# A Macaron block with routed experts: routing steps one to a unit, projections earlier, expert passes shifted

## The chip, the cores and the metric

The kernel runs on one core of a Trainium2 chip. The metric is the device time of one execution in microseconds, the median of several runs. In this text PE is TensorE's matmul side and PEld its weight loads, DVE is VectorE, ACT is ScalarE, POOL is GpSimd and SP is SyncE.

## What is computed

Eight sequences of 512 tokens with 128 features go through a feed-forward half, an attention and a second feed-forward half with the same weights:

```python
x = x + 0.5 * _L0_ffn_ref(_layernorm(x), ...)
x = x + _L0_attn_ref(_layernorm(x), w_qkv, w_o, log_xi)
x = x + 0.5 * _L0_ffn_ref(_layernorm(x), ...)      # the same weights as the first
```

The feed-forward part is a mixture of 8 experts of width 512, of which each token takes the best 2:

```python
logits = jnp.einsum('bsd,de->bse', x, router_w) + router_b
topk_scores, topk_idx = jax.lax.top_k(logits, 2)
topk_gates = jax.nn.softmax(topk_scores, axis=-1)
...
    h = jax.nn.relu(jnp.einsum('bsd,df->bsf', x, w1) + bb1)      # for each expert
    y = jnp.einsum('bsf,fd->bsd', h, w2) + bb2
    acc = acc + y * c[..., None]                                 # c: the token's gate, or 0
```

The attention is causal, with 16 heads of width 8, a rotation on some head types and a distance decay on others. All is float32.

## The kernel before

**Groups and rooms.** Tokens are sent to their experts through DRAM. The sequences form three groups ahead of the attention (f0: 0 and 1; f1: 2 to 4; f2: 5 to 7) and three behind it (g0: 0 to 2; g1: 3 to 5; g2: 6 and 7). For each group, `route` finds every token's two experts and its place, and 8 scatters a sequence (GpSimd's indirect DMA, line 796) write the normalised tokens to `xs`. `experts` fetches each expert's rows from `xs` (line 854), transposes them (867), multiplies by W1 (876), applies ReLU (883, or 885 on VectorE), multiplies by W2 (900), adds the bias (904) and writes `ys` (907). `combine` gathers each token's two results (968) and adds them to `x` with the gates (955).

**Routing in six steps.** `route` is a generator. Where the layernorm isn't there yet it takes three steps. Then come: 1, four transposes into one PSUM bank and their copy `xnT` by VectorE (713, 715); 2, the router's matmuls (742) and VectorE's comparison of each logit with each other (746 to 760); 3, rank and mask (763, 765); 4, the count of earlier tokens by matmuls on the mask (770 to 778), the places, and the entry of the eight scatters in the queue of transfers; 5 and 6, the gates.

**Units.** The program is an order written out by hand: PE, ACT, DVE and SP run their instructions as they are issued. Time is cut into numbered units. Units 0 to 95 each hold one step of attention: sequence b, group g of four heads, step s of three; a sequence is 12 units. `surround(n, att)` (1278) issues one unit: the scores of unit n (1059) and their exponentials (1066), the values of unit n-1 (1085), one piece of expert work, the causal minimum (1073), one transfer, the outputs, the additions due, then all streams due in this unit, each followed by its share of expert pieces, and a second transfer if the queue is long or holds an urgent one. The units before 0 and after 97 have no attention in them. An expert pass of a group is 65 or 73 pieces; a piece is one transposition, one W1 product of a block or one W2 product of a tile. The pieces of a pass are spread evenly over the units that `plan` gives it (1272): (group, unit of the fetch, first unit, end).

**Streams.** `at(u, stream, steps, each)` (1256) puts `each` steps of a stream into each unit from u on. `routed` puts the three steps of a layernorm into a unit each, then the six of the routing two to a unit: transposes with the router's matmuls, mask with the count, the gates together. `project(b)` has nine steps: layernorm, transposes, the projection's matmuls in two parts, the rotation on GpSimd in two parts, and the copies into `qpad` and `kpad` (1023, 1026). `operands(b, g)` transposes one head group of `qpad` and `kpad` into `qT` and `kT` (1036, 1042), in two steps. `finish(b)` ends the attention of b, and the routing for the second half begins two units after that.

**Buffers.** In units 0 to 97, PSUM has four banks for scores, one for values, and three named `m` that all else takes in turn: expert pieces, transposes, the router's logits, counts, outputs. The queue of transfers holds scatters and gathers in order; each is also held back until the last marked instruction issued before it is done (`behind_mark`).

**The start.** Sequences 0, 1 and 2 are normalised and routed by a list of steps ahead of the first unit (lines 1326 to 1335). Sequence 3 is normalised there, and routed in unit `first`, together with the first expert's pieces.

Of the kernel before, what the change touches and what calls it, by code (L numbers as in the profile page):

```python
# [22 lines left out]
T = N // P  # L23
# [452 lines left out]
class Main:  # L476
# [127 lines left out]
    def behind_mark(self, ins):  # L604
        if self.mark is not None:
# [3 lines left out]
                reason="transfers kept apart",  # L609
            )  # L610

    def transfer(self, second=False):

        if self.jobs and (
            not second or len(self.jobs) > 4 or any(urgent for urgent, _ in self.jobs)
        ):
            self.jobs.popleft()[1]()
# [108 lines left out]
        g.seen = const.tile([P, E], BF, name=f"seen_{key}")  # L726
        return g

    def route(self, g, i, urgent=False):

        nc, small, tc = self.nc, self.small, self.tc
        b = g.seqs[i]
# [71 lines left out]
            self.behind_mark(ins)  # L804
            g.placed += 1

        for t in range(T):
            for r in range(2):
                self.jobs.append((urgent, partial(scatter, t, r)))

        with nc.allow_low_precision(reason="counts of at most 32, exact in bf16"):
            by_e = mask.rearrange("p t e -> p e t")
# [133 lines left out]
    def combine(self, g, i, dst=None, urgent=False, ahead=False):  # L946

        nc = self.nc
        b = g.seqs[i]
        x = self.x[b]  # L950
        self.whole[b] = False

        def add(t, yts):
            for r in range(2):
                nc.vector.scalar_tensor_tensor(  # L955
                    x[:, t, :], yts[r], g.gates[:, i, t, r : r + 1], x[:, t, :],
                    ALU.mult, ALU.add,
                )
            if t == T - 1:
                self.whole[b] = True  # L960
                if dst is not None:
                    nc.sync.dma_start(dst[b].rearrange("(t p) d -> p t d", p=P), x)

        yts = {}

        def gather(t, r):
            yt = self.yp.tile([P, D], FP, tag=f"yt{r}", name=f"yt_{g.key}_{b}_{t}_{r}")
            self.pool.indirect_dma_start(
                out=yt[:, :], out_offset=None, in_=g.ys[:, :],
                in_offset=bass.IndirectOffsetOnAxis(  # L970
                    ap=g.back[:, i, t, r : r + 1], axis=0
                ),
            )
            yts[t, r] = yt
            if r == 1:
                self.adds.append((self.unit + 2, partial(add, t, [yts[t, 0], yts[t, 1]])))

        new = [(urgent, partial(gather, t, r)) for t in range(T) for r in range(2)]
        if ahead:
            self.jobs.extendleft(reversed(new))  # L980
        else:
            self.jobs.extend(new)
        yield


# [144 lines left out]
    def verdict(self, bad):  # L1130

        nc = self.nc
        nr = B * G * T * 4
        flat = self.recs.rearrange("p b g t h -> p (b g t h)")
        spare = self.p1.tile([P, T * 3 * D], FP, tag="qkv", name="spare")
        okay, wok = spare[:, : nr + 3 * D], spare[:, nr + 3 * D : nr + 6 * D]
        nc.vector.tensor_scalar(okay[:, :nr], flat, 1.0 / SUM_LIMIT, None, ALU.is_ge)
        nc.vector.scalar_tensor_tensor(
            okay[:, :nr], flat, SUM_LIMIT, okay[:, :nr], ALU.is_le, ALU.mult
        )  # L1140
        nc.vector.tensor_scalar(wok, self.wqkv_sb, -W_LIMIT, None, ALU.is_ge)
        nc.vector.scalar_tensor_tensor(
            okay[:, nr:], self.wqkv_sb, W_LIMIT, wok, ALU.is_le, ALU.mult
        )
        cnt = self.const.tile([P, 1], FP, name="okay_cnt")
        nc.vector.tensor_reduce(cnt, okay, AX.X, ALU.add)
        cp = self.bank([P, 512], "okay_ps")
        nc.tensor.matmul(cp[:1, :1], cnt, self.ones_f, start=True, stop=True)
        over = self.const.tile([1, 1], FP, name="over")
        nc.vector.tensor_reduce(  # L1150
            over, self.counts.rearrange("o k e -> o (k e)"), AX.X, ALU.max
        )
        nc.vector.tensor_scalar(over, over, 0.5, None, ALU.is_gt)
        nc.vector.scalar_tensor_tensor(
            bad, cp[:1, :1], float(P * (nr + 3 * D)) - 0.5, over, ALU.is_lt, ALU.max
        )


@with_exitstack
def macaron_kernel(  # L1160
# [22 lines left out]
    bad = flags.tile([1, 1], I32, name="bad")  # L1183

    def run(*streams):
        for s in streams:
            for _ in s:
                pass
# [23 lines left out]
    with ExitStack() as main:  # L1212
        m = Main(tc, main, aps)
# [4 lines left out]
        f0 = m.open_group([0, 1], 384, 0, "f0")  # L1218
        f1 = m.open_group([2, 3, 4], 512, 1, "f1")
        f2 = m.open_group([5, 6, 7], 512, 2, "f2")  # L1220
        g0 = m.open_group([0, 1, 2], 512, 1, "g0")
        g1 = m.open_group([3, 4, 5], 512, 2, "g1")
        g2 = m.open_group([6, 7], 384, 0, "g2")
        order = [f0, f1, f2, g0, g1, g2]
        place = {True: {}, False: {}}
# [13 lines left out]
        def step(*streams):  # L1239
            for st in streams:  # L1240
                next(st, None)
# [8 lines left out]
        units = [(b, g, s) for b in range(B) for g in range(G) for s in range(len(m.STEPS))]  # L1250
        per = len(m.STEPS)
        seq = G * per
        first, core, tail, ends = -28, len(units), 111, 127
        due = {}

        def at(u, stream, steps, each=1):

            for k in range(0, steps, each):
                due.setdefault(u + k // each, []).append((stream, min(each, steps - k)))

        def routed(u, g, i, urgent=False):
            r = m.route(g, i, urgent)
            if g is not f1:
                at(u, r, 3)
                u += 3
            at(u, r, 6, 2)

        def combined(u, g, i, dst=None, urgent=False, ahead=False):
            at(u, m.combine(g, i, dst, urgent, ahead), 1)


        plan = [
            (f0, first, first, -15), (f1, -17, -15, 7), (f2, 5, 7, 41), (g0, 50, 52, 86),
            (g1, 85, 87, tail - 1), (g2, tail - 2, tail - 1, ends),
        ]
        fills = {}

# [46 lines left out]
        with m.banks(("m", 8)):  # L1324

            n = [m.normalise(b) for b in range(5)]
            r = [m.route(f0, 0), m.route(f0, 1), m.route(f1, 0)]
            step(n[0], n[0], n[1], n[1], n[0], n[0])
            step(r[0], n[1], n[1], r[0], r[1], r[0], r[0])
            transfers(8)  # L1330
            step(r[1], r[1], r[1], n[2], n[2], n[3], n[3], n[4], n[4])
            transfers(8)
            step(r[0], r[0], r[1], r[1], n[2], n[2], r[2], n[3], n[3], r[2], n[4], n[4], r[2], r[2])
            transfers(8)
            run(*r, *n)
            m.bias_columns()

            routed(first, f1, 1, urgent=True)
            routed(first + 2, f1, 2, urgent=True)
            routed(first + 1, f2, 0, urgent=True)  # L1340
            combined(-15, f0, 0, urgent=True, ahead=True)
            routed(-15, f2, 1, urgent=True)
            combined(-11, f0, 1)
            routed(-8, f2, 2, urgent=True)
            at(-9, m.project(0), 9)
            at(-1, m.operands(0, 0), 2, 2)
            for b in range(B):
                u = b * seq
                if b == 2:
                    combined(8, f1, 0, urgent=True)  # L1350
                elif b > 2:
                    combined(u - (19 if b == 5 else 20), *place[True][b], urgent=b == 5)
                if b > 0:
                    at(u - (9 if b == 1 else 10), m.project(b), 9)
                for g in range(G):
                    v = u + g * per
                    if g == 0 and b > 0:
                        at(v - 1, m.operands(b, g), 2, 2)
                    elif g > 0:
                        at(v - 2, m.operands(b, g), 2)  # L1360
                at(u + seq + 2, m.finish(b), 2)
                routed(u + seq + 4, *place[False][b], urgent=b in (2, 5, 7))
            for i in range(3):
                combined(87, g0, i, out, urgent=True)
                combined(tail, g1, i, out, urgent=True)

            for u in range(first, 0):
                surround(u, False)
                if u == first:
                    m.attention_constants()  # L1370
                    m.load_x(5, 6, 7)
                    m.clear(2)
        with m.banks(("st", 1), ("o", 1), ("m", 3)):
            for u in range(core + 2):
# [1 line left out]
        with m.banks(("m", 8)):  # L1376
            for u in range(core + 2, ends):
                surround(u, False)
                if u == tail:
                    m.verdict(bad)  # L1380
            run(fills["g2"][0])
            assert not due, due
            for i in range(2):
                run(m.combine(g2, i, out))
            m.mark = None
            while m.jobs:
                m.transfer()
                m.unit += 1
                m.additions()
            m.unit += 2  # L1390
            m.additions()
# [53 lines left out]
```

## Time and profile before

| | |
|---|---|
| time, median of 3 runs | 830.54 us (830.22 to 835.65) |
| span of the profiled run | 828.3 us |
| the chain that ended last, by engine | PE 74%, DVE 13%, DMA 4%, POOL 3%, issue 3%, ACT 2% |
| first and second product of the experts, busy | 199.8 us (876), 196.1 us (900) |
| scores and values, busy | 103.8 us (1059), 93.4 us (1085) |
| exponentials, busy | 158.7 us (1066) |
| indirect transfers on GpSimd, busy, the four costliest groups | 231.2 us |

The profile cuts the span into 40 slices of 20.7 us. Each digit is the share of a slice in tenths, 9 standing for 90% or more; PEclk is the TensorE clock that was granted.

```profile
PE   3178999789989789889969879979989979978950
DVE  6645135534345555654675545656645454522322
PEclk9999999989989889889978989989999999998985
```

PE starts slowly in the first two slices, is near full from the fourth on, and is done before the last. Its clock dips in many of the slices in between. The slices about number 20 (400 to 440 us) are the attention units that have no expert pieces in them.

### The profile page before, as it was taken

The numbers are of one execution on the slowest core, as the hardware profiler recorded it, in microseconds if no ns is written. First come the engines' busy times: TensorE is split into PE (matmuls) and PEld (weight loads), VectorE is DVE, ScalarE is ACT, GpSimd is POOL, SyncE is SP. The second block draws the span as 40 slices with busy tenths as digits, with TensorE's granted clock in tenths as the row PEclk, the third lists the DMA queues.
The fourth block names the chain that finished last, engine by engine and source line by source line (L and its number), as shares of the span: only waits on it lengthen the run. The fifth ranks groups of instructions, "written<-read, shape, count | busy, mean of one in ns | idle before, by whom it ended". The sixth has DMA issues, their size and how long they took to land.

```text
span 828.3 us, 12920 instructions
## 1 busy us (share of the span) xinstructions
PE 683.3 (82%) x4867; PEld 432.9 (52%) x4867; DVE 409.8 (49%) x1351; ACT 346.3 (42%) x520; POOL 317.2 (38%) x352
## 2 busy tenths in 40 slices
PE   3178999789989789889969879979989979978950
PEld 2157766556555446546524545545646546755840
DVE  6645135534345555654675545656645454522322
ACT  4023434345636245345435435534545535323410
POOL 4743556540232242243362233324214224542734
PEclk9999999989989889889978989989999999998985
DMA  9762333111211010101102011101002112322522
GB/s 298 242 215 67 102 97 102 39 39 52 58 46 32 14 45 26 29 27 32 33 23 78 17 35 46 45 10 36 21 13 77 52 45 77 103 87 64 134 70 64
DMA packets 74005, 55.77 MB, mean 67 GB/s; under 512 B 7088, under 2 KB 66768, under 8 KB 73936
## 3 DMA queue, kind: packets, MB, share of 16 engines
q1 hardware_dynamic: 65456, 38.08, 15.5%
q0 software_dynamic: 8192, 16.79, 7.0%
q8 instruction: 40, 0.66, 0.3%
q14 instruction: 29, 0.24, 0.1%
q10 hardware_dynamic: 288, 0.01, 0.0%
HBM read 27.07 MB, written 27.79 MB: 66 GB/s over the span
## 4 chain that ended last, share of the span: by engine, by line
PE 74%; DVE 13%; DMA 4%; POOL 3%; issue 3%; ACT 2%; POOLq 0%; DVEq 0%; SPq 0%
PE st L1059 11%; PE z_g L876 10%; PE y_g L900 10%; PE y_f L900 10%; PE z_f L876 9%; PE o L1085 9%; PE qkv_ps_a L998 3%; DVE ee L1073 3%; DVE x L955 2%; PE qT_ps L1036 2%; PE kT_ps L1036 1%; DMA yt_g<-ys,back_g 1%; PE xbT_ps_g L867 1%; PE otok_ps L1103 1%; PE lg_ps_f L742 1%
## 5 line engine op out<-in xcount | busy, mean ns | idle before, releaser
L1066 ACT ACTIVATE ee<-st 128x768 f32<-128x768 f32 (+1 forms) x192 | 158.7, 879 | 97.0 <-PE st L1059 96.8
L467 POOL DMA_INDIRECT yt_f<-ys,back_f x64 | 64.6, 1009 | 177.7 <-DVE ee L1073 81.4
L1059 PE MATMUL st<-qT,kT 32*128 32x512 f32 (+3 forms) x1024 | 103.8, 499 | 13.5 <-DVE qT L1042 7.5
L900 PEld LDWEIGHTS y_f<-w_sb,h_f 128*128 128x128 f32 x704 | 94.0, 200 | 33.9 <-issue 20.7
L900 PEld LDWEIGHTS y_g<-w_sb,h_g 128*128 128x128 f32 x704 | 89.9, 193 | 34.9 <-issue 18.9
L796 POOL DMA_INDIRECT xs<-xn_g,to_g x64 | 65.5, 1023 | 100.6 <-DVE ee L1073 60.6
L876 PE MATMUL z_f<-xT_f,w_sb 128*128 128x512 f32 (+1 forms) x192 | 100.4, 612 | 2.0 <-DVE ysb_f L904 1.3
L876 PE MATMUL z_g<-xT_g,w_sb 128*128 128x512 f32 (+1 forms) x192 | 99.4, 605 | 1.9 <-DVE ysb_g L904 1.3
L1073 DVE TENSOR_TENSOR ee<-ee,keep 128x256 f32<-128x256 f32 (+1 forms) x192 | 92.3, 505 | 16.6 <-ACT ee L1066 16.6
L900 PE MATMUL y_f<-w_sb,h_f 128*128 128x128 f32 x704 | 100.1, 288 | 0.0
L467 POOL DMA_INDIRECT yt_g<-ys,back_g x64 | 61.8, 965 | 92.2 <-ACT h_g L883 32.9
L900 PE MATMUL y_g<-w_sb,h_g 128*128 128x128 f32 x704 | 96.0, 281 | 0.8 <-ACT h_g L883 0.8
L1085 PE MATMUL o<-ee,vpad 128*32 128x512 f32 (+3 forms) x1024 | 93.4, 461 | 0.0
L883 ACT ACTIVATE h_f<-z_f,b1T 128x512 f32<-128x512 f32 (+1 forms) x82 | 53.0, 646 | 91.5 <-PE z_f L876 91.3
L883 ACT ACTIVATE h_g<-z_g,b1T 128x512 f32<-128x512 f32 (+1 forms) x82 | 52.9, 645 | 74.6 <-PE z_g L876 74.2
L904 DVE TENSOR_TENSOR ysb_g<-y_g,b_sb 128x128 f32<-128x128 f32 x88 | 25.5, 289 | 117.0 <-PE y_g L900 116.9
L904 DVE TENSOR_TENSOR ysb_f<-y_f,b_sb 128x128 f32<-128x128 f32 x88 | 25.3, 288 | 106.8 <-PE y_f L900 102.9
L1059 PEld LDWEIGHTS st<-qT,kT 32*128 32x128 f32 x1024 | 45.9, 195 | 60.8 <-issue 27.7
L1085 PEld LDWEIGHTS o<-ee,vpad 128*32 128x32 f32 x1024 | 24.4, 112 | 56.6 <-issue 30.8
L796 POOL DMA_INDIRECT xs<-xn_n,to_f x40 | 39.3, 982 | 34.1 <-ACT h_f L883 11.5
L1042 ACT COPY kT<-kT_ps 128x512 f32<-128x512 f32 x32 | 18.8, 589 | 54.1 <-PE kT_ps L1036 54.1
L876 PEld LDWEIGHTS z_f<-xT_f,w_sb 128*128 128x128 f32 x192 | 32.5, 207 | 14.7 <-issue 9.5
(174 smaller groups left out, 816.7 us busy)
## 6 DMA issues: line engine op xcount, KB each, us to landing
w_sb<-in_L_ffn_W_dram SPq DMA_DIRECT2D x16, 256.0 KB, 5.8
xs<-zeros SPq DMA_DIRECT2D x2, 2048.0 KB
xb_f<-xs SPq DMA_DIRECT2D x16, 256.0 KB, 3.7
ys<-ysb_f SPq DMA_DIRECT2D x16, 256.0 KB, 2.4
xb_g<-xs SPq DMA_DIRECT2D x16, 256.0 KB, 3.0
ys<-ysb_g SPq DMA_DIRECT2D x16, 256.0 KB, 2.4
x<-in_L_attn_x_dram SPq DMA_DIRECT2D x8, 256.0 KB, 4.4
out_dram<-x SPq DMA_DIRECT2D x8, 256.0 KB, 2.6
```

What stands on the lines that cost most here:

```text
L467: ins = op(*args, **kw)
L796: ins = nc.gpsimd.indirect_dma_start(out=g.xs[:, :], out_offset=bass.IndirectOffsetOnAxis(ap=g.to[:, i, t, r : r + 1], axis=0), in_=xn[:, ...
L876: nc.tensor.matmul(z[:, :n], self.w1_sb[:, e, ts(c, P)], xT[:, n0 : n0 + n], start=True, stop=True,)
L883: ins = nc.scalar.activation(dst, z[:, :n], AF.Relu, bias=bias)
L900: nc.tensor.matmul(y, h[:, c, ts(t, P)], self.w2_sb[:, e, c, :], start=(c == 0), stop=(c == C - 1),)
L904: ins = nc.vector.tensor_tensor(ys[:, t, :], y, self.b2_sb[:, e], ALU.add)
L998: nc.tensor.matmul(pp[:, : 3 * D], xnT[:, ts(t, P)], self.wqkv_sb, start=True, stop=True)
L1036: self.nc.tensor.transpose(tp[:, ts(t, P)], pad[:, t, 4 * g : 4 * g + 4, :].rearrange("p h s -> p (h s)"), self.ident,)
L1059: nc.tensor.matmul(st[:, h, c0 : c0 + N - kt * P], kT[r0 : r0 + SLOT, ts(kt, P)], qT[r0 : r0 + SLOT, kt * P :], start=True, stop=True,)
L1066: nc.scalar.activation(ee[:, two, :width], st[:, two, :width], AF.Exp)
L1073: ins = self.nc.vector.tensor_tensor(d, d, self.keep.unsqueeze(1).unsqueeze(1).to_broadcast([P, 2, len(parts), P]), ALU.min,)
L1085: self.nc.tensor.matmul(self.o[h * SLOT : (h + 1) * SLOT, kt * P :], self.vpads[b % 2][:, kt, 4 * g + h, :], ee[:, h, c0 : c0 + n], start= ...
```

## The change

Only the order of the work changes. No operation of the computation is added or taken out.

- `routed` gives each of the six routing steps a unit of its own, so that the copies and masks that the next matmuls read are made a unit ahead of them. A routing's scatters enter the queue two units later.
- The projections begin a unit or two earlier, and the operands of the first head group are made in the two units ahead of their scores, as for the other groups.
- `first`, `tail`, `ends`, the plan of the expert passes, the combines and their places in the queue are moved to match.
- The fourth sequence (3, the second of f1) is routed as far as its scatters in the list ahead of the first unit. The loads of x for sequences 5 to 7 go ahead of the first expert's fetch.
- The verdict on overflow is issued in two units rather than one.
- The code that enters transfers in the queue is shared by `route` and `combine`; a routing may now go ahead of what is queued.

```diff
+    def enter(self, transfers, urgent, ahead):
+        new = [(urgent, transfer) for transfer in transfers]
+        if ahead:
+            self.jobs.extendleft(reversed(new))
+        else:
+            self.jobs.extend(new)
...
-    def route(self, g, i, urgent=False):
+    def route(self, g, i, urgent=False, ahead=False):
...
-        for t in range(T):
-            for r in range(2):
-                self.jobs.append((urgent, partial(scatter, t, r)))
+        self.enter([partial(scatter, t, r) for t in range(T) for r in range(2)], urgent, ahead)
...
         nc.vector.tensor_reduce(cnt, okay, AX.X, ALU.add)
+        yield
         cp = self.bank([P, 512], "okay_ps")
...
-        first, core, tail, ends = -28, len(units), 111, 127
+        first, core, tail, ends = -29, len(units), 113, 129
...
-        def routed(u, g, i, urgent=False):
-            r = m.route(g, i, urgent)
+        def routed(u, g, i, urgent=False, ahead=False):
+            r = m.route(g, i, urgent, ahead)
             if g is not f1:
                 at(u, r, 3)
                 u += 3
-            at(u, r, 6, 2)
+            at(u, r, 6)
...
-            (f0, first, first, -15), (f1, -17, -15, 7), (f2, 5, 7, 41), (g0, 50, 52, 86),
-            (g1, 85, 87, tail - 1), (g2, tail - 2, tail - 1, ends),
+            (f0, first, first, -16), (f1, -18, -16, 6), (f2, 4, 6, 43), (g0, 52, 54, 89),
+            (g1, 87, 89, tail - 1), (g2, tail - 2, tail - 1, ends),
...
-            r = [m.route(f0, 0), m.route(f0, 1), m.route(f1, 0)]
+            r = [m.route(f0, 0), m.route(f0, 1), m.route(f1, 0), m.route(f1, 1, True)]
...
-            run(*r, *n)
+            step(r[2], r[2], r[3], r[3], r[3], r[3])
+            run(*r[:3], *n)
             m.bias_columns()
-
-            routed(first, f1, 1, urgent=True)
-            routed(first + 2, f1, 2, urgent=True)
-            routed(first + 1, f2, 0, urgent=True)
-            combined(-15, f0, 0, urgent=True, ahead=True)
-            routed(-15, f2, 1, urgent=True)
-            combined(-11, f0, 1)
-            routed(-8, f2, 2, urgent=True)
-            at(-9, m.project(0), 9)
+            m.load_x(5, 6, 7)
+
+            at(first, r[3], 2)
+            routed(first, f1, 2, urgent=True)
+            routed(first, f2, 0, urgent=True)
+            combined(-16, f0, 0, urgent=True, ahead=True)
+            routed(-17, f2, 1, urgent=True)
+            combined(-13, f0, 1)
+            routed(-10, f2, 2, urgent=True)
+            at(-10, m.project(0), 9)
             at(-1, m.operands(0, 0), 2, 2)
             for b in range(B):
                 u = b * seq
                 if b == 2:
-                    combined(8, f1, 0, urgent=True)
+                    combined(6, f1, 0, urgent=True, ahead=True)
                 elif b > 2:
-                    combined(u - (19 if b == 5 else 20), *place[True][b], urgent=b == 5)
+                    combined(u - (17 if b == 5 else 21), *place[True][b], urgent=b == 5, ahead=b == 5)
                 if b > 0:
-                    at(u - (9 if b == 1 else 10), m.project(b), 9)
+                    at(u - 11, m.project(b), 9)
                 for g in range(G):
-                    v = u + g * per
-                    if g == 0 and b > 0:
-                        at(v - 1, m.operands(b, g), 2, 2)
-                    elif g > 0:
-                        at(v - 2, m.operands(b, g), 2)
+                    if b + g > 0:
+                        at(u + g * per - 2, m.operands(b, g), 2)
                 at(u + seq + 2, m.finish(b), 2)
-                routed(u + seq + 4, *place[False][b], urgent=b in (2, 5, 7))
+                routed(u + seq + 4, *place[False][b], urgent=b in (2, 5, 6, 7), ahead=b == 7)
             for i in range(3):
-                combined(87, g0, i, out, urgent=True)
+                combined(89, g0, i, out, urgent=True)
                 combined(tail, g1, i, out, urgent=True)
+            at(tail, m.verdict(bad), 2)
 
             for u in range(first, 0):
                 surround(u, False)
                 if u == first:
                     m.attention_constants()
-                    m.load_x(5, 6, 7)
                     m.clear(2)
...
-                if u == tail:
-                    m.verdict(bad)
```

More of the change, by code (lines that the diff above doesn't have):

```diff
@@ L976, in gather @@
                 self.adds.append((self.unit + 2, partial(add, t, [yts[t, 0], yts[t, 1]])))
[L978 to L982, printed above, removed]
+        self.enter([partial(gather, t, r) for t in range(T) for r in range(2)], urgent, ahead)
         yield
@@ L1156, in verdict @@
         )
+        yield
 @with_exitstack
```

## The prediction

> **What bounds the kernel now.** I read the busy shares first, then the waits of TensorE, then two stretches side by side, then the timeline of one routing.
>
> ```profile
> PE 683.3 (82%) x4867; PEld 432.9 (52%) x4867; DVE 409.8 (49%) x1351; ACT 346.3 (42%) x520; POOL 317.2 (38%) x352
> core 0: 828.3 us, clock 0.925
> ```
>
> TensorE (PE) is the only engine near full, and the clock it was granted averages 0.925. The waits of PE (us in total, times, longest):
>
> ```profile
> PE pos_ps_g L770 <- DVE mask_g L765: 22.5, 8, 3.8
> PE xnT_ps_f L713 <- DVE xn_n L698: 18.5, 2, 11.5
> PE lg_ps_g L742 <- DVE xnT_g L715: 14.6, 8, 2.4
> PE pos_ps_f L770 <- DVE mask_f L765: 13.3, 7, 3.6
> PE qT_ps L1036 <- DVE qpad L1023: 7.8, 2, 5.2
> PE st L1059 <- DVE qT L1042: 7.5, 6, 1.8
> PE lg_ps_f L742 <- DVE xnT_f L715: 7.2, 7, 1.4
> PE okay_ps L1148 <- DVE over L1150: 3.6, 1, 3.6
> ```
>
> Four of the eight rows are the routing, 57.6 us together; each is PE waiting for a VectorE result made in the same unit. What that does to a stretch (columns: PE, PEld, DVE, ACT, POOL busy; granted clock; DMA):
>
> ```profile
> 243.50:265.80 22.30, 22.30 (x197) 13.50 (x196) 14.47 (x48) 12.88 (x18) 3.08 (x4) 1.00 0.12 31
> 270.90:293.00 22.10, 15.96 (x101) 10.16 (x100) 11.73 (x32) 4.57 (x7) 5.07 (x7) 0.81 0.04 10
> 797.80:828.30 30.50, 0.00 (x0) 0.00 (x0) 5.94 (x17) 0.00 (x0) 15.22 (x16) 0.53 0.22 60
> ```
>
> The first holds units 13 to 17: five units with expert pieces and no routing, PE full, full clock, 4.5 us a unit. The second holds two routing units and a little more: PE idle 6.1 us and the clock at 0.81. The third is the end, after the last matmul. Inside the second:
>
> ```profile
> 270.87 0.93 PE L1059 MATMUL st<-qT,kT 32*128 32x384 f32 x8
> 274.12 0.60 PE L713 MATMUL xnT_ps_g<-ident,xn_g 128*128 128x128 f32 x4
> 276.36 0.68 DVE L715 COPY xnT_g<-xnT_ps_g 128x512 f32<-128x512 f32 x1
> 277.09 1.37 PE L742 MATMUL lg_ps_g<-rw_sb,xnT_g 128*128 128x8 f32 x8 [2.38 <-DVE xnT_g L715]
> 282.42 0.94 PE L1059 MATMUL st<-qT,kT 32*128 32x256 f32 x16
> 285.89 1.28 DVE L1073 TENSOR_TENSOR ee<-ee,keep 128x512 f32<-128x512 f32 x2
> 288.20 0.41 DVE L763 TENSOR_REDUCE rank_g<-gt_g 128x32 f32<-128x256 f32 x1
> 288.64 0.25 DVE L765 TENSOR_SCALAR mask_g<-rank_g 128x32 bf16<-128x32 f32 x1
> 288.95 0.21 PE L770 MATMUL pos_ps_g<-mask_g,earlier 128*128 128x32 bf16 x1 [3.77 <-DVE mask_g L765]
> 291.81 2.09 PE L1059 MATMUL st<-qT,kT 32*128 32x512 f32 x8
> ```
>
> The three score rows start units 19, 20 and 21: two units take 20.9 us. The copy and the mask are short (0.68 and 0.66 us); they come late because VectorE is in the middle of the unit's causal minima and additions. PE stands behind them with expert pieces queued that need neither.
>
> **What the Trainium skill says.** "PSUM — Partial Sum Buffer", Engine vs sequencer instructions: ScalarE, VectorE and GpSimd queues are strict FIFO, and matmuls start in program order. The timeline agrees: lg and pos stop everything behind them for 2.38 and 3.77 us. "TensorE: Matmul & The Clock Gate", Part 1: the clock is either full or half, chosen from recent activity in windows of about 3.4 us. The 0.81 beside a full 1.00 agrees, and here waits of 2 to 4 us are enough, less than a whole idle window for some. "Perfetto Trace Analysis", Optimization Strategy: find the gaps of the most-contended engine and make their dependencies start sooner. The same page, Matmuls: independent groups should rotate through PSUM banks so that evacuation overlaps the next group. In the core only three banks rotate, so a late VectorE read can still stop PE; the trace has this twice (z behind ysb at 300 and 495 us, 1.3 us each).
>
> **The change part by part.**
> (a) One routing step per unit. Copy xnT goes into the unit before lg, mask into the unit before pos. No instruction is added. Each result then has the rest of its unit, 2 us and more of expert pieces, and the next unit's scores, values and first piece, about 3 us more: against waits of at most 3.8 us. Of the 57.6 us, 10.0 us are in the prologue before 43 us (0.8, 2.2, 2.7, 0.8, 3.6), where the order of the first three sequences stays. Two more (0.8 and 1.6 us, the fourth sequence) move to (f). That leaves 45.2. VectorE still does the same work, 1.9 us for the comparison chain (0.19 and four of 0.42) in the unit of lg, and holds PSUM banks of pieces behind it; at 0.3 to 0.5 us for each of 20 or so steps I leave 8 us in. Gain 37. Cost on GpSimd: the scatters enter the queue two units later; counting two transfers a unit, they still finish 4 units before the f1 fetch, 4 before f2, 1 or more before g0, g1 and g2, as before.
> (b) Projection sooner. The 7.8 us of qT behind qpad (5.2 for sequence 0, 2.7 for 1) came from writing qpad in the unit that transposes it. Now a unit or more lies between. Gain 7.
> (c) Operands of head group 0 in two units rather than one. qT is copied a unit earlier; kT, copied by ScalarE, now stands just ahead of the scores, as it does for the other groups, whose st waits for kT are 2.8 us in five. Of 10.3 us (7.5 and 2.8) gain 4.
> (d) The verdict in two units: okay_ps no longer waits for its own count. Gain 3 of 3.6; its work moves by nothing else.
> (e) Clock. A mean of 0.925 means 62 us of clock missing in 828.3; the last 30.5 us at 0.53 hold 14 of it and have no matmul. So 48 us in the body. The stretch without expert pieces, 397.5 to 446, has clock 0.79 and so 10 of it, and is partly held by the exponentials there; I count it in (g). From the remaining 38: some lies under idle time already counted[...], so 80%, 30. It hangs on the waits of (a), (b), (d); the wait for the g2 fetch (4.0 us, DMA) and some small gaps stay. I take three quarters: 22.
> (f) Fourth sequence in the prologue. Its transposes, lg and pos (1.1, 1.9, 0.2 us of PE) run where PE waited 4.1 us for the first expert's rows. The chain there, after VectorE has ended the third sequence's gates at 41.0 us: copy 0.7, lg 1.9, VectorE 2.5, pos 0.6, about 47.2 against the 42.75 us at which the first expert's transposes start now: 4.4 us later. It takes out 3.2 us of PE work and 2.4 us of waits behind that. Gain 1. The loads of x for 5 to 7 go ahead of the first fetch on SyncE, which stood idle from 34 to 40 us with the DMA share at 0.20 from 35 to 40: hidden.
> (g) Units 41 to 51 carry no pieces and took 52 us, of which waits of (a) and (c) are 6. The first two ran 3.4 us, 11 times that plus 3 us of routing is 40. Beyond the 6, gain 5.
> Plan bounds, three more units, reordered combines: the pieces and their matmuls are the same 4867, a unit has no cost of its own, and the combine of sequence 5 keeps two units from gather to addition. Nothing.
> Sum: 37 + 7 + 4 + 3 + 22 + 1 + 5 = 79. 830.5 - 79 = 751.5, so **751 us**.
>
> **Rivals.**
> R1, waits turn into new ones: VectorE, 65% busy in a unit of 4.5 us (14.47 of 22.30), holds one of three banks in most of the spread steps, and half the gain goes: about 790. For it: the two z behind ysb waits. Against: units 13 to 17 held a projection's copies with no gap.
> R2, the clock stays low because smaller gaps are enough for it: the waits go, the clock and (g) do not: 751 + 27 = 778. For it: a wait of 1.3 us at 118 us already has 0.87 beside it (115 to 128). Against: full units keep 1.00.
> R3, slower: a later scatter or the tighter combine of sequence 5 (additions end in the unit in which its projection starts, where one gather already held VectorE 2.3 us at 424) stops VectorE, and PE with it, at several boundaries, and the first expert starts later still. At 10 us for each of five fetches and the prologue, with half the gain: 830 - 40 + 60 = 850.
>
> **How the numbers follow.** Forecast 0.66, R1 0.15, R2 0.13, R3 0.04, the rest (better than the sum, all waits and clock gone: 740 and below) 0.02 beyond its own spread. The low end takes the 8 us left in (a), and the quarter of clock left in (e): 751 - 16, 733 with a little of (c). The high end, 787, takes in R2 and the better half of R1. Faster by over 1%: all but R3 and a sliver, 0.94; within 1% 0.02; slower 0.04.
>
> **What would show it.** Right: waits of pos_ps_g and lg_ps_g under 3 us each, qT behind qpad and okay_ps under 1, mean clock 0.95 or more, routing units near 5 us, PE busy around 640 us since fewer matmuls run at half clock. Wrong: new rows of z, y or o behind DVE results of over 15 us in total (R1); waits gone with the clock at 0.93 (R2); waits for xb or x rows (R3).

## The result and the profile after

The changed kernel took 772.63 us (median of 4 runs, 771.14 to 774.20). The ratio to the kernel before is 0.9275, with a 95% interval of 0.9230 to 0.9321. The kernel before took 833.09 us beside it (median of 4 runs). The forecast was 751 us, in a range of 733 to 787: faster as forecast, inside the range, and 22 us above the forecast. Run again with later experiments beside it, the same kernel took 759.40 us, ratio 0.9181 (0.9102 to 0.9261).

The kernel before itself moved from one set of runs to the next: 829 to 837 us beside the first four experiments (two_steps, split_alone, kt_first, fillers), 817 to 828 beside the next four, 817 to 830 beside the last four. The first four ran on one chip, the other eight on a second, where the kernel before has two levels: 817 to 822 us at a mean clock of 0.937 to 0.947, and 827 to 830 us at 0.925 to 0.927, as in its profile (828.3 us, 0.925). So differences are read between kernels that ran together, or from ratios.

First the busy shares and the mean clock of the changed kernel:

```profile
PE 657.7 (85%) x4867; PEld 419.7 (54%) x4867; DVE 419.3 (54%) x1359; ACT 339.6 (44%) x512; POOL 316.8 (41%) x352
core 0: 772.5 us, clock 0.961
```

The same 4867 matmuls keep PE busy for 25.6 us less (683.3 to 657.7). The trace's record of the clock says why: ahead of the last matmul, half clock was granted in 19 stretches of the kernel before, 95.2 us together, and in 6 of the changed one, 34.0 us. (The record begins at 52 and at 60 us; the views count what lies ahead as full clock.) PE's idle time, span less busy, went from 145.0 to 114.8 us, or 30.2 less. The two make up the 55.8 us by which the span fell. The waits of PE that bear on the sum (total, times, longest), without those for xnT_ps_f at the start:

```profile
PE st L1060 <- ACT kT L1043: 19.3, 12, 5.1
PE pos_ps_f L777 <- DVE mask_f L772: 12.0, 4, 3.6
PE z_f L881 <- ACT xT_f L874: 5.6, 2, 4.9
PE z_g L881 <- DVE xnT_g L722: 3.9, 2, 2.8
PE y_f L905 <- DVE xnT_g L722: 2.3, 2, 1.2
PE qT_ps L1037 <- DVE qpad L1024: 2.1, 1, 2.1
```

The rows of pos_ps_g and lg_ps_g, 37.1 us before, are gone. What is left of the first-half routing lies in the start. In the place of the old list a new one leads: the scores wait for kT, 19.3 us where it was 2.8.

The stretch that now holds units 19 to 22 (columns: PE, PEld, DVE, ACT, POOL busy; clock; DMA):

```profile
252.70:274.80 22.10, 20.43 (x177) 11.46 (x176) 18.71 (x44) 10.70 (x15) 7.97 (x11) 1.00 0.13 37
```

22.1 us hold four units and a little more, where two filled 20.9 us. PE is idle for 1.7 us, not 6.1, and the clock is full. But VectorE is busy for 18.7 us of 22.1, where it was 11.7 (4.8 us of it is a hold, shown below).

### The profile page after: what moved, and what is told of

It is laid out like the page before. It is cut to its first block, busy times and chain, and to the rows that moved or that the text cites. A ratio compares the mean times of both kernels' runs of the same rounds, so it can differ in the third digit from the quotient of the medians.

```text
span 772.5 us, 12905 instructions
## 1 busy us (share of the span) xinstructions
PE 657.7 (85%) x4867; PEld 419.7 (54%) x4867; DVE 419.3 (54%) x1359; ACT 339.6 (44%) x512; POOL 316.8 (41%) x352
## 4 chain that ended last, share of the span: by engine, by line
PE 72%; DVE 13%; issue 4%; ACT 3%; POOL 2%; DMA 2%; another core or an unknown queue 2%; POOLq 0%; DVEq 0%; ACTq 0%
PE st L1060 11%; PE y_g L905 10%; PE z_g L881 10%; PE o L1086 10%; PE y_f L905 10%; PE z_f L881 9%; DVE ee L1074 3%; DVE x L960 2%; PE qkv_ps_a L999 2%; DVE eq_g L763 1%; PE kT_ps L1037 1%; PE xbT_ps_g L872 1%; DMA yt_g<-ys,back_g 1%; PE otok_ps L1104 1%
## 5 line engine op out<-in xcount | busy, mean ns | idle before, releaser
L1060 PE MATMUL st<-qT,kT 32*128 32x512 f32 (+3 forms) x1024 | 100.4, 485 | 22.1 <-ACT kT L1043 19.3
L905 PEld LDWEIGHTS y_f<-w_sb,h_f 128*128 128x128 f32 x704 | 90.6, 194 | 36.1 <-issue 18.8
L881 PE MATMUL z_f<-xT_f,w_sb 128*128 128x512 f32 (+1 forms) x192 | 97.7, 597 | 6.4 <-ACT xT_f L874 5.6
L881 PE MATMUL z_g<-xT_g,w_sb 128*128 128x512 f32 (+1 forms) x192 | 96.0, 587 | 7.8 <-DVE xnT_g L722 3.9
L905 PE MATMUL y_f<-w_sb,h_f 128*128 128x128 f32 x704 | 96.9, 282 | 2.8 <-DVE xnT_g L722 2.3
L467 POOL DMA_INDIRECT yt_g<-ys,back_g x64 | 61.4, 959 | 70.3 <-ACT h_g L888 15.5
L888 ACT ACTIVATE h_g<-z_g,b1T 128x512 f32<-128x512 f32 (+1 forms) x80 | 51.2, 645 | 88.1 <-PE z_g L881 70.5
L888 ACT ACTIVATE h_f<-z_f,b1T 128x512 f32<-128x512 f32 (+1 forms) x77 | 49.4, 642 | 68.7 <-PE z_f L881 57.3
L803 POOL DMA_INDIRECT xs<-xn_n,to_f x40 | 39.2, 980 | 34.4 <-issue 10.2
L881 PEld LDWEIGHTS z_g<-xT_g,w_sb 128*128 128x128 f32 x192 | 30.5, 197 | 22.3 <-issue 8.6
```

What stands on the lines that cost most here:

```text
L467: ins = op(*args, **kw)
L803: ins = nc.gpsimd.indirect_dma_start(out=g.xs[:, :], out_offset=bass.IndirectOffsetOnAxis(ap=g.to[:, i, t, r : r + 1], axis=0), in_=xn[:, ...
L881: nc.tensor.matmul(z[:, :n], self.w1_sb[:, e, ts(c, P)], xT[:, n0 : n0 + n], start=True, stop=True,)
L888: ins = nc.scalar.activation(dst, z[:, :n], AF.Relu, bias=bias)
L905: nc.tensor.matmul(y, h[:, c, ts(t, P)], self.w2_sb[:, e, c, :], start=(c == 0), stop=(c == C - 1),)
L1060: nc.tensor.matmul(st[:, h, c0 : c0 + N - kt * P], kT[r0 : r0 + SLOT, ts(kt, P)], qT[r0 : r0 + SLOT, kt * P :], start=True, stop=True,)
```

## The experiments

### The split of the steps, undone and alone

```diff
-            at(u, r, 6)
+            at(u, r, 6, 2)
```

> The changed kernel with the routing steps again two to a unit, all else of the change kept. If the split of the steps carries the gain: the waits of the count for the mask and of the router for its transposes come back (about 45 us outside the start) with the half clock behind them (about 18 us), less some 10 us as the gates' exponential moves away from the copy kT: about 820 us (808 to 832). If the earlier projections and operands carry it: under 790 us, with few routing waits.

This undoes the split in the changed kernel. Measured: 817.41 us, ratio 0.9817 (0.9769 to 0.9865), so 45 us over the changed kernel at its first run. The waits are back:

```profile
PE lg_ps_g L749 <- DVE xnT_g L722: 24.9, 8, 4.8
PE pos_ps_g L777 <- DVE mask_g L772: 18.8, 7, 3.0
PE st L1060 <- ACT kT L1043: 6.0, 7, 2.5
```

The waits for kT fell from 19.3 to 6.0 us; the gates' exponential had left kT's unit. The other direction, the split alone in the kernel before:

```diff
             r = m.route(g, i, urgent)
+            each = 1 if g.key[0] == "g" and g.seqs[i] in (0, 1, 3, 4, 6) else 2
...
-            at(u, r, 6, 2)
+            at(u, r, 6, each)
```

> The kernel before, with the six routing steps one to a unit in five of the eight second-half routings (sequences 0, 1, 3, 4, 6, where the transfers still come in time), nothing else moved. If the split alone carries the gain: each of the five loses about 6 us of waits and 2 to 3 us of half clock, about 793 us (785 to 803), with waits of pos_ps_g and lg_ps_g down to three times each. If the split needs the earlier projections: above 815 us.

Measured: 790.90 us, ratio 0.9476 (0.9425 to 0.9528), 43.8 us below the kernel before beside it: 8.8 us for each of five routings. pos_ps_g kept three waits (6.3 us), lg_ps_g three (3.4 us). The split carries most of the gain, with the projections left where they were.

### The queue ahead of kT

```diff
-        def at(u, stream, steps, each=1):
+        def at(u, stream, steps, each=1, early=False):
...
-                due.setdefault(u + k // each, []).append((stream, min(each, steps - k)))
+                todo = due.setdefault(u + k // each, [])
+                todo.insert(0 if early else len(todo), (stream, min(each, steps - k)))
...
-                        at(u + g * per - 2, m.operands(b, g), 2)
+                        at(u + g * per - 2, m.operands(b, g), 2, early=True)
```

What suggested it is the timeline of the changed kernel at the end of unit 23:

```profile
276.03 0.60 PE L1037 MATMUL kT_ps<-ident,kpad 128*128 128x128 f32 x4
276.43 1.28 DVE L1074 TENSOR_TENSOR ee<-ee,keep 128x512 f32<-128x512 f32 x2
277.63 0.73 DVE L960 SCALAR_TENSOR_TENSOR x<-yt_f,gates_f,x 128x128 f32<-128x128 f32 x2
278.50 0.19 DVE L829 TENSOR_TENSOR ex_g<-lg_g,top_g 128x32 f32<-128x32 f32 x1
278.72 0.23 ACT L832 ACTIVATE ex_g<-ex_g 128x32 f32<-128x32 f32 x1 [2.83 <-DVE ex_g L829]
278.86 0.57 ACT L1043 COPY kT<-kT_ps 128x512 f32<-128x512 f32 x1
279.48 1.14 PE L1060 MATMUL st<-qT,kT 32*128 32x512 f32 x8 [2.42 <-ACT kT L1043]
```

kT's transposes are done at 276.6 us, and ScalarE is idle. Ahead of the copy in its queue stands the exponential of routing step 5. It waits for VectorE, which first does the causal minima and the additions. The split had moved step 5 from the unit U-3 into U-1, the unit of kT. A queue that is served in order passes VectorE's lateness on to PE by way of ScalarE. The exponential stands directly ahead of the copy in 6 of the 12 waits, which make 15.7 of the 19.3 us; the other 6 make 3.6 us, near the 2.8 us of before.

> The changed kernel with one edit: among the streams due in a unit, the operands qT and kT come first, so that ScalarE's copy kT no longer stands behind the gates' exponential, which waits for VectorE. If that queue makes the new waits of the scores for kT (19.3 us, 12 times): they fall under 6 us, with some half clock, about 756 us (750 to 762). If PE only meets the next late result there (exponentials, causal minima): 767 us or more, with new waits of the scores or values of like size. The start is the same as in the changed kernel: if the slow stretch of PE from 47 to 53 us belongs to the program, it shows again.

Measured: 755.87 us, ratio 0.9061 (0.9018 to 0.9104), with the interval clear of the changed kernel's at its first run (0.9230 to 0.9321).

```profile
PE st L1060 <- ACT kT L1043: 4.4, 4, 2.1
PE z_g L881 <- DVE qT L1043: 3.9, 2, 2.8
PE y_f L905 <- DVE qT L1043: 2.3, 2, 1.2
```

14.9 us of waits for kT went, PE was busy 3.3 us less (657.7 to 654.4), and the time fell by 16.8. The second and third row stayed, to the tenth, under another name (they were behind xnT_g): that is another cause.

### The rotation that holds VectorE

The timeline of the changed kernel shows it:

```profile
263.95 2.79 DVE L763 TENSOR_TENSOR eq_g<-lg_g 128x256 f32<-128x256 f32 x1
264.36 0.73 POOL L467 TENSOR_TENSOR r_a<-qkv_a,rope_sb 128x256 f32<-128x256 f32 x1
265.03 1.42 POOL L467 TENSOR_TENSOR qkv_a<-r_a,r_a 128x256 f32<-128x256 f32 x2
```

One comparison of the router, 0.42 us long elsewhere, lasts 2.79 us: from its start until 0.3 us after the profile's end of GpSimd's three operations of the rotation (GpSimd's spans are rough). The Trainium skill has this in "SBUF — State Buffer", Who interferes with whom: a VectorE instruction with two SBUF inputs contends with a GpSimd instruction that reads SBUF. The trace agrees, and the hold lasted for three GpSimd operations in a row rather than one. In the changed kernel 5 of the 8 comparisons (line 763) are held so, and 4 pairs of the additions to x (line 960), each pair for 2.4 us; in the kernel before it was no comparison and one pair. With the split undone it is no comparison and 4 pairs, with the shift of the projections undone (below) 5 comparisons and no pair: the split put the comparisons under the rotation, the shift the additions. The experiments put the rotation on VectorE:

```diff
-        self.pool.tensor_tensor(r[0], t1, cos, ALU.mult)
+        nc.vector.tensor_tensor(r[0], t1, cos, ALU.mult)
...
```

and the same for the five operations after it.

First on top of the edit for kT:

> The changed kernel with the operands first in their unit, and the projection's rotation on VectorE rather than GpSimd (six operations, about 2.5 us a projection). VectorE operations with two inputs ran 2.4 us too long beside each GpSimd stretch (23 us in all). If PE's remaining waits for VectorE (z, y and o behind xnT, qT, ee, ysb, about 12 us) come from that: they fall under 5 us, 747 us (743 to 751). If VectorE's own 20 us more of work delay it as much: 755 us or more.

Measured: 725.33 us, ratio 0.8825 (0.8767 to 0.8883), the lowest of all, with the interval clear of those of the changed kernel and of the edit for kT alone. VectorE has 48 instructions more and is busy for less: 412.4 us against 419.2 with the edit for kT alone. The same comparison, in the view of its tile (durations least, median, most, in ns):

```profile
L763 DVE TENSOR_TENSOR eq_g<-lg_g x8: 416/2770/2802, 264.0 to 670.6; 128x256 f32<-128x256 f32 x8
L763 DVE TENSOR_TENSOR eq_g<-lg_g x8: 417/418/421, 251.8 to 624.5; 128x256 f32<-128x256 f32 x8
```

The first line is the changed kernel, the second this one. Its leading waits outside the start are st behind ee, 3.7 us, and the fetch for g2, 2.6 us; the mean clock is 0.979. Then the rotation alone, beside the changed kernel, and in the kernel before:

> The changed kernel as it is, beside the three others on one chip. The last four ran beside runs of the kernel before at 819 us, the first four at 831 to 835 us, so small differences between the two sets can't be read. If the slow stretch of PE at 47 to 53 us belongs to the program: 770 to 774 us with first scores at 161 us, as at first. If it comes and goes: about 765 us, first scores at 155 us, a wait for xT_f under 2 us.

> The changed kernel with the rotation on VectorE and the operands in their place behind the gates' step. If GpSimd's hold of VectorE is a second loss, apart from the queue ahead of kT: 20 us or so below the changed kernel beside it, with the waits for kT still over 12 us. If it is what makes kT late: 35 us or more below, kT under 6 us.

> The kernel before with the rotation on VectorE. In it VectorE ran too long by 16 us beside GpSimd's rotation, in many short operations rather than two long ones a sequence. If the hold hurts only where the changed order has put comparisons and additions beside the rotation: within 6 us of the kernel before. If it was part of the routing's waits all along: 12 us or more below it.

Measured: 759.40 us for the changed kernel, 747.93 us with the rotation on VectorE (ratio 0.9034, 0.8952 to 0.9116). That is 11.5 us less, where I expected 20, with the waits for kT at 16.4 us, as beside it (16.5). So the two losses are separate: neither edit removes the other's wait. What went between these two is z and y behind xnT_g (6.2 to 0.4 us), o behind ee (1.3 to 0) and qT behind qpad (2.1 to 0). The last is the rotation's own result, which may come sooner with or without a hold. GpSimd's time for transfers (281 us busy, not 316) isn't the gain: the wait for fetched rows stayed (2.5 and 2.6 us). In the kernel before the edit gave 816.93 us, ratio 0.9874 (0.9787 to 0.9960). The runs of the kernel before beside it stand on both of its levels, two at 817 to 819 us and four at 828 to 830, so whether this is 12 us or next to nothing is not settled; its waits fell by 2.3 us (pos_ps_g) and 2.6 us (qT).

### The clock by itself

```diff
+    def filler(self, bank, key, n):
+
+        if key[0] == "g":
+            for _ in range(n):
+                self.nc.tensor.matmul(
+                    bank[:, 128:384], self.ident, self.w1_sb[:, 0, :256], start=True, stop=True
+                )
...
+        self.filler(lp, key, 8)
...
+        self.filler(pp, key, 12)
```

The fillers stand ahead of the router's matmuls and of the count's in the kernel before. They give PE work while it waits; what those matmuls need of VectorE comes no sooner.

> The kernel before, with matmuls of constants that nobody reads put ahead of the router's matmuls (8 of 128x256) and of the count (12) in the eight second-half routings: PE works through most of each wait, and the waits themselves stay. If half clock follows the waits and slows the work after them: 815 us (810 to 820), mean clock 0.95. If it costs next to nothing, or has another cause: 828 to 835 us.

Measured: 842.98 us, ratio 1.0114 (1.0066 to 1.0162). The size was wrong: the 20 fillers of a routing stand in the trace as 40 matmuls and took 9.0 us, where its two waits were 4.6.

```profile
core 0: 840.5 us, clock 0.964
L733 PE MATMUL pos_ps_g<-w_sb,ident 128*128 128x256 f32 x192 | 42.9, 380 | 0.0
L733 PE MATMUL lg_ps_g<-w_sb,ident 128*128 128x256 f32 x128 | 29.4, 382 | 0.0
```

72.3 us of fillers stand in 37.1 us of waits, and the kernel got slower by 1%. PE was busy for 726.5 us; less the fillers that is 654.2, against 683.3 for the same matmuls in the kernel before. Hence half as many, 4 and 6:

> The kernel before with half as many filler matmuls as the run with fillers (4 ahead of the router's, 6 ahead of the count, about 1.9 and 2.7 us), so that they end inside the waits of 2.4 and 3.8 us. The long fillers ran 72 us in place of 37 us of waits, and the span rose by 12 us, so some 23 to 29 us were saved in all other matmuls. If that is the clock: 808 us (803 to 813), the fillers' rest of the waits in place and the clock at 0.95 or more. If the long run's saving came from something else: 825 us or more.

Measured: 807.00 us, ratio 0.9829 (0.9769 to 0.9890), or 12 us below its neighbour; the four runs, 806.7 to 807.2, lie below all eleven of the kernel before, 817 to 828. PE was busy for 688.8 us, of which 37.6 were fillers (22.1 and 15.5): 651.2 for the program's own matmuls, 32.1 less than in the profile of before. The scores that take 2.09 us at 291.81 us in the kernel before, behind the count's wait, stand here as

```profile
286.54 1.14 PE L1069 MATMUL st<-qT,kT 32*128 32x512 f32 x8
```

The record of the clock has 30.6 us of half clock ahead of the last matmul, and 34.0 with the long fillers, where it had 95.2. Half of what went is 32.3 and 30.6 us, and PE's own matmuls ran 32.1 and 29.1 us shorter. So work that does nothing made the kernel faster, because more of the matmuls behind the waits then ran at full clock. "TensorE: Matmul & The Clock Gate", Part 1, says that recent activity sets the clock; this shows what it is worth here. The 29 to 32 us are against the profile at 0.925, though. At 0.945, as in most runs of the kernel before beside the short fillers, some 16 us less of clock is missing (an estimate: 0.020 of 820 us). That leaves about 16 us, near the 12 us of time.

Whether a wait costs clock depends on where it falls. Four stretches of 3.4 us of the changed kernel (columns as before), laid on the grid on which the half-clock stretches of its record begin and end:

```profile
274.84:278.25 3.41, 2.22 (x20) 1.79 (x16) 1.99 (x5) 1.06 (x2) 1.47 (x2) 1.00 0.06 19
278.25:281.66 3.41, 2.18 (x25) 1.03 (x26) 0.41 (x3) 2.10 (x4) 1.30 (x2) 1.00 0.13 42
339.64:343.05 3.41, 1.56 (x20) 0.63 (x24) 1.19 (x6) 0.99 (x3) 1.86 (x2) 1.00 0.32 96
343.05:346.47 3.42, 3.42 (x19) 2.00 (x12) 0.79 (x2) 2.13 (x3) 0.10 (x1) 0.50 0.06 19
```

Two waits of 2.42 us for kT end at 279.48 and 341.49 us. The first is divided between two stretches, PE is busy for 65% and 64% of them, and the clock stays full. More of the second falls into one, PE is busy for 46% of it, and the next has half clock. All six half-clock pieces of this kernel ahead of its last matmul follow a stretch with PE busy for 46% or less, and last 3.4, 6.8 or 10.2 us. In the kernel before, 14 of 19 follow one of 48% or less but five one of 60 to 71%, so this is not the whole rule.

### The fourth sequence, and the shift of the projections

```diff
-            step(r[2], r[2], r[3], r[3], r[3], r[3])
-            run(*r[:3], *n)
+            run(*r, *n)
...
-            at(first, r[3], 2)
-            routed(first, f1, 2, urgent=True)
+            at(first, m.route(f1, 1, True), 6, 2)
+            at(first + 2, m.route(f1, 2, True), 6, 2)
```

> The changed kernel with the fourth sequence routed in the first units again (two steps to a unit, as the fifth), all else kept. The prediction had the move to the start gain 1 us: then about 774 us. If the start lost by it (a wait of 4.9 us for the first expert's xT and 7.4 us of later full clock stand against 3.2 us of work and 2.4 us of waits): about 767 us (764 to 770), with the first expert's transposes at about 43 us and its first full clock near 52 us again.

This routes the fourth sequence in the units again, and also the fifth with two steps to a unit. Measured: 764.83 us, ratio 0.9325 (0.9277 to 0.9373): no faster than the changed kernel, by the ratios (0.9275, and 0.9181 when run again). So the suspicion that the start lost by the move fell. This kernel's first scores start at 161.3 us, the second line here; the kernel with the projections late, beside it and with the changed start, has them at 156.1 (third line). The changed kernel at its first run (first line) had 161.5, and 155.7 when run again.

```profile
L1060 PE MATMUL st<-qT,kT x1024: 267/481/1218, 161.5 to 638.1; 32*128 32x512 f32 x43, 32*128 32x256 f32 x43, 32*128 32x128 f32 x43, 32*128 32x384 f32 x42
L1060 PE MATMUL st<-qT,kT x1024: 267/481/1074, 161.3 to 632.3; 32*128 32x512 f32 x43, 32*128 32x256 f32 x43, 32*128 32x128 f32 x43, 32*128 32x384 f32 x42
L1060 PE MATMUL st<-qT,kT x1024: 267/480/1218, 156.1 to 623.5; 32*128 32x512 f32 x43, 32*128 32x256 f32 x43, 32*128 32x128 f32 x43, 32*128 32x384 f32 x42
```

So the move, with the fifth sequence's steps, gains about 5 us (764.83 against 759.40 on the same chip), and at the first run something took them back. In the first run's start:

```profile
47.71 0.90 PE L872 MATMUL xbT_ps_f<-ident,xb_f 128*128 128x128 f32 x3
52.99 0.36 SPq L858 DMA_DIRECT2D xb_f<-xs  x1
53.00 0.48 ACT L874 COPY xT_f<-xbT_ps_f 128x384 f32<-128x384 f32 x1 [13.05 <-remote]
```

and when run again:

```profile
46.75 0.90 PE L872 MATMUL xbT_ps_f<-ident,xb_f 128*128 128x128 f32 x3
47.68 0.36 SPq L858 DMA_DIRECT2D xb_f<-xs  x1
47.69 0.48 ACT L874 COPY xT_f<-xbT_ps_f 128x384 f32<-128x384 f32 x1 [7.79 <-PE xbT_ps_f L872]
```

Two engines that wait for the same transposes start together, 4.4 us after the end that the profile models in the first run, at once in the second. VectorE, too, reads the count (posb_f) 2.0 us after its modelled end there. PE was probably slower than the profile shows; that only its signals came late is not excluded. It was so in the changed kernel's first profile and in those of two_steps and kt_first, which ran on the first chip, and in none of the later ones, on the second. So it can be the chip; the record doesn't name that of the first run. What slowed it stays open.

Then the shift of the projections and of the first operands is undone, with all else kept:

```diff
-                    at(u - 11, m.project(b), 9)
+                    at(u - (9 if b == 1 else 10), m.project(b), 9)
...
+                    if g == 0 and b > 0:
+                        at(v - 1, m.operands(b, g), 2, 2)
```

> The changed kernel with the projections and the operands of the first head group where they were before (projections one or two units later, qT and kT both in the unit ahead of their scores), all else kept. If the shift is worth what the prediction said (2.7 of the 7 us of (b), as sequence 0 stays early, and 4 of (c)): 779 us (775 to 784), with qT behind qpad 2.7 us and the scores' waits for qT back. If the shift gave nothing, because kT lost on ScalarE what qT gained: 770 to 774 us.

> The changed kernel with projections and first operands where they were before: once more, beside the changed kernel. If the shift of projections and operands made PE slower (kT behind the gates' exponential in its own unit, rotation under the router's comparisons): 6 us or more below the changed kernel beside it. If the earlier run owed its 754 us to the chip and the start: within 4 us, or above by 5 as the prediction had it.

Measured: 754.49 us (0.9201, 0.9143 to 0.9260), and then, beside the changed kernel's 759.40, 754.70 us (0.9110, 0.9028 to 0.9192). The four runs of the second, 751.4 to 754.9, all lie below the four of the changed kernel, 758.3 to 759.8, though the intervals of the ratios overlap. The shift took 5.3 us off the wait of qT for qpad (7.4 to 2.1 us) and put 5.9 us on the scores' for kT (10.6 to 16.5). It also brought the 6.2 us of z and y behind xnT_g, with the additions that it put under the rotation. Once the steps are split, the shift as made cost some 5 us, where (b) and (c) had it gain; it was not tried together with the edit for kT.

## Why the prediction was right, and where it was short

Each step of the sum against the first run, in us:

| step | predicted | measured | from |
|---|---|---|---|
| (a) routing waits outside the start, less new waits | 37 | 34.5 | 45.2 gone; z, y, o behind VectorE 13.3 (rows of 0.5 and more), before 2.6 |
| (b) qT behind qpad | 7 | 5.7 | 7.8 to 2.1 |
| (c) operands of the first head group | 4 | -9.0 | 10.3 to 19.3 |
| (d) verdict | 3 | 3.6 | row gone |
| (e), (g) clock | 27 | 25.6 | PE busy 683.3 to 657.7 |
| (f) start | 1 | -4.4 | waits of the start 35.0 to 39.4 |

The measured column sums to 56.0; the span fell by 55.8. (Rows not in the table, of 1.4 us and less each, about cancel.) The waits of the start are, before, 18.5 (xnT_ps_f) + 10.0 + 2.4 (routing) + 4.1 (xb_f); after, 11.4 + 7.0 (xnT_ps_f) + 12.0 (pos_ps_f) + 4.1 (lg_ps_f, 2.5, 0.8 and 0.8) + 4.9 (xT_f).

**Right.** The mechanism and its main sizes. The split is worth 45 us undone, and 44 us alone in five routings. The clock term, which no row of the waits gives, came out within 2 us of the profile at 0.925, and the fillers show it apart from the waits; against a run of the kernel before at 0.945 it would be some 16 us less. (a), (b) and (d) are within 3 us each. Of the signs, the waits of the router and of the count, okay_ps, the clock (0.961) and the routing units (four of them in 20.7 us) came as forecast. Two did not: qT still waits 2.1 us for qpad, and PE is busy for 657.7 us, not around 640 (the sum's own 27 us of clock would make it 656).

**Wrong: (c).** It put kT "just ahead of the scores, as it does for the other groups". It looked at the unit and not at the queue: in the same unit the split had placed the gates' exponential ahead of kT on ScalarE. The strict order of the queues, which the prediction cites, was seen at PE but not asked of ScalarE. The term missed by 13 us, 15.7 us of waits stand behind the exponential, and the edit that only swaps the order brought the time down by 16.8 us, with the clock behind the waits. The stretch of (g), eleven units without pieces, felt it too: it took 45.4 us, not 40, with one of these waits, 5.1 us, in it and 10.2 us of half clock from 394 us on.

**Mis-sized: (f).** The chain of the fourth sequence came as worked out (47.2 us forecast for the first expert's transposes, 47.7 and 46.8 measured). The first run's slow stretch took 4.9 us that the later ones don't have. When run again the waits of the start were 34.0 us (18.4 + 11.1 + 4.0 + 0.5), 1 us less than before, and the first scores came 5.6 us sooner than with the fourth sequence late. So the term was 1 us by the sum, a loss at the first run and about 5 us later.

**Misread.** R3 laid a VectorE addition of 2.3 us over its length at 424 us to a gather. It was the rotation:

```profile
424.08 3.03 DVE L955 SCALAR_TENSOR_TENSOR x<-yt_f,gates_f,x 128x128 f32<-128x128 f32 x2
424.47 0.74 POOL L467 TENSOR_TENSOR r_a<-qkv_a,rope_sb 128x256 f32<-128x256 f32 x1
425.15 1.42 POOL L467 TENSOR_TENSOR qkv_a<-r_a,r_a 128x256 f32<-128x256 f32 x2
```

The new waits that (a) allowed 8 us for were 10.7, and most have this cause: with the rotation on VectorE alone, the rows of z, y and o behind VectorE fell from 11.3 to 4.0 us. What is left, o_tok above all, is of another kind.

**The rivals.** R1, waits that turn into new ones, is half of what happened, though mainly by ScalarE's queue and GpSimd's hold and not by the count of banks: 16.5 us more behind kT and 10.7 behind VectorE, against 62 us of waits gone. R2 is ruled out: the clock rose to 0.961, and half clock fell from 95.2 to 34.0 us. R3 did not come: the waits for fetched rows are 2.6 us (xb), less than before.

## What to carry to other kernels

When a step is moved so that its result comes early, write down for each engine what then stands ahead of what in that unit: a short operation that waits for a busy engine holds everything behind it in its own queue. A wait of PE costs itself and, often, half clock behind it: of the 56 us gained here, 26 were clock (fewer against the kernel before at its lower level), and even filling the waits with idle matmuls paid, as long as the fillers ended with the waits. Before moving work to an idle engine, ask whether it shares something with a busy one: taking the six operations of each rotation back from GpSimd made VectorE less busy.

## What the runs showed of the hardware

- A VectorE operation with two SBUF inputs (0.42 us alone) lasted 2.79 us when it started just ahead of three GpSimd operations on SBUF; once these were gone, the longest of the eight was 0.42 us.
- Half clock came in pieces of 3.4, 6.8 and 10.2 us. Of two PE waits of 2.42 us in the changed kernel, the one that left PE busy for 46% of a stretch of 3.4 us brought it, the one divided between two stretches (65% and 64% busy) did not. With the waits filled, it fell from 95.2 to 34.0 and 30.6 us.
- In three profiles of eight with this start, the engines that waited for one group of transposes began 3.0 to 4.4 us after its modelled end; in the other five at once. What waits for a matmul tells when its result was there.
- The same kernel took 772.6 and 759.4 us on two occasions, with ratios to its neighbours of 0.9275 and 0.9181.
